# A layer of RWKV attention and a mixture of experts: expert tiles added to the output in DRAM, instead of written aside and gathered

## The chip, the cores and the metric

The kernel runs on one core of one Trainium2 chip. The metric is the device time of one execution in microseconds, the median of several runs. The profile is one execution with the hardware profiler; its times are microseconds from the first instruction, unless marked ns. The engines are TensorE (PE, with its weight loads PEld), VectorE (DVE), ScalarE (ACT), GpSimd (POOL) and SyncE (SP). Each of them works through its own queue of instructions in order. SyncE, ScalarE and GpSimd also issue DMA transfers.

## The reference

For 2048 tokens of 512 float32 numbers, the output is the input, plus an attention branch, plus a branch of routed experts. Both branches read the same normalised input.

```python
x = L0_attn_x                      # (1, 2048, 512)
xn = layernorm(x)
out = x + attention(xn) + experts(xn)

# attention: a recurrence over all tokens for each of 512 channels
# (tokens are 8 sequences of 256 only in the weights' setup; here one sequence of 2048)
r, v, k = split(xn @ W_rvk.T)
# step over t, with w = -exp(time_decay), u = time_first:
#   no = max(o, u + k);  A = exp(o - no);  Bc = exp(u + k - no)
#   y = (A * p + Bc * v) / (A * q + Bc)
#   no2 = max(w + o, k); p, q, o updated in the same manner with w
attention = (sigmoid(r) * y) @ W_out.T

# experts: 8 routed ones and 4 that return their input, the best 2 of 12 for each token
probs = softmax(xn @ classifier_w.T)
_, idx = top_k(probs + bias, 2)
rw = probs[idx] * 1.5
experts = sum over the 2 of: rw * (silu(xn @ gate.T) * (xn @ up.T)) @ down.T    # routed
                         or  rw * xn                                            # the other 4
```

## The kernel before

The kernel has five stages. It normalises x in four blocks of 512 tokens, stores the normalised rows (xs) in DRAM, and transposes each block. It computes the router and sorts tokens by expert: every expert gets whole tiles of 128 places, at most 40 tiles, of which the first 25 are always computed. It runs 16 units of the recurrence (wkv), one for each block and quarter of the channels. Between them it runs the expert tiles: each fetches its weights, gathers its 128 rows of xs by index, and stores 128 rows into ys in DRAM. After a branch for tiles 25 to 39, it combines: each tile of 128 tokens gathers two rows per token from ys, weighs and adds them to x and to the output projection. A scheduler decides the order in which each engine's instructions stand, so that the order of the text is a priority and not the order on the chip.

The pools, and the loads of x at the start:

```python
    xyp = pool("xy", 5)
    ewp = pool("ew", 3)
    rows = pool("rows", 4)
    rp = pool("route", 1)
    small = pool("small", 2)
    kvp = pool("kv", 2)
    wk = pool("wk", 2)
    ex_p = pool("exp", 2)
    # ...
    xs = dram.tile([T, C], F32, tag="xs", name="xs")
    ys = dram.tile([MAX_TILES * P, C], F32, tag="ys", name="ys")

    def load_x(i):
        t = rows.tile([P, C], F32, tag="ra", name=f"x{i}")
        nc.sync.dma_start(t, x[i * P : (i + 1) * P, :])
        xt[i] = t

    for i in range(NJ):
        load_x(i)
    # ... (classifier, bias, decay, first; constants on GpSimd)
```

The normalisation, the transposes and the router of one block, and the order of the loads:

```python
    def norm(b):
        js = slice(b * NJ, (b + 1) * NJ)
        for j in range(NJ):
            i = b * NJ + j
            st = small.tile([P, 6], F32, tag="st", name=f"st{i}")
            nc.vector.bn_stats(st, xt[i])
            nc.vector.bn_aggr(mv[:, i, :], st)
        var = mv[:, js, 1]
        ve = small.tile([P, NJ], F32, tag="ve", name=f"ve{b}")
        nc.vector.tensor_scalar_add(ve, var, EPS)
        # ... (variance, square root, reciprocal: rstd and shift)
        xn = []
        for j in range(NJ):
            i = b * NJ + j
            t = rows.tile([P, C], F32, tag="rb", name=f"xn{i}")
            nc.vector.tensor_scalar(t, xt[i], mv[:, i, 0:1], rstd[:, i : i + 1], ALU.subtract, ALU.mult)
            nc.scalar.dma_start(xs[i * P : (i + 1) * P, :], t)
            xn.append(t)
        xnT[b] = xyp.tile([P, CC, TB], F32, tag="xy", name=f"xnT{b}")
        for c in range(CC):
            pt = ps_tr.tile([P, TB], F32, tag="tr", name=f"pt{b}_{c}")
            for j in range(NJ):
                nc.tensor.transpose(pt[:, j * P : (j + 1) * P], xn[j][:, c * P : (c + 1) * P], ident)
            nc.scalar.copy(xnT[b][:, c, :], pt)
        for j in range(NJ):
            for c in range(CC):
                nc.tensor.matmul(
                    pl[:, b * NJ + j, :],
                    xnT[b][:, c, j * P : (j + 1) * P],
                    cls_sb[:, c, :],
                    start=(c == 0),
                    stop=(c == CC - 1),
                )

    norm(0)
    # ...
    for b in range(1, NTB):
        for j in range(NJ):
            load_x(b * NJ + j)
        if b == 1:
            load_w(2)
        norm(b)
    load_w(1)
    load_w(0)
    # ... (blank tiles of ys written from ACT's queue; the load of wout_sb)
```

The lists of tokens by place, after the choice of experts and the places (slot, low, high) are known; xa and xb carry what the input itself adds to the output:

```python
    NK = 2 * NT
    lowhot = xyp.tile([P, NK, P], BF16, tag="xy", name="lowhot")
    nc.vector.tensor_tensor(
        lowhot,
        lane.unsqueeze(1).to_broadcast([P, NK, P]),
        low.rearrange("p k j -> p (k j)").unsqueeze(2).to_broadcast([P, NK, P]),
        ALU.is_equal,
    )
    # ... (hh: is_equal of 40 tiles with high_b)
    tok = rp.tile([P, NK, 2, MAX_TILES], BF16, tag="tok", name="tok")
    nc.vector.tensor_tensor(
        tok[:, :, 0, :],
        hh,
        tok_j.rearrange("p k j -> p (k j)").unsqueeze(2).to_broadcast([P, NK, MAX_TILES]),
        ALU.mult,
    )
    nc.vector.tensor_scalar(tok[:, :, 1, :], hh, tok_p, None, ALU.mult)
    pi = ps_o.tile([P, 2, MAX_TILES], F32, tag="o", name="pi")
    for k in range(NK):
        nc.tensor.matmul(pi, lowhot[:, k, :], tok[:, k], start=(k == 0), stop=(k == NK - 1))
    pis = rp.tile([P, 2, MAX_TILES], F32, tag="pis", name="pis")
    nc.vector.tensor_copy(pis, pi)
    token_i = const.tile([P, MAX_TILES], I32, tag="token_i", name="token_i")
    nc.vector.scalar_tensor_tensor(token_i, pis[:, 0], float(P), pis[:, 1], ALU.mult, ALU.add)
    # ... (which expert a tile is of; wts, zero, xa, xb)
```

The expert tiles:

```python
    def fetch(i):
        # ... (e: the tile's expert)
        w = ewp.tile([P, CC, 2 * INTER], F32, tag="gw", name=f"gw{i}")
        nc.sync.dma_start(w, gu[bass.ds(e, 1)].rearrange("o p c n -> p (o c) n"))
        d = ewp.tile([P, IC, C], F32, tag="dw", name=f"dw{i}")
        nc.sync.dma_start(d, down[bass.ds(e, 1)].rearrange("o p c n -> p (o c) n"))
        xg = rows.tile([P, C], F32, tag="ra", name=f"xg{i}")
        nc.gpsimd.indirect_dma_start(
            out=xg,
            out_offset=None,
            in_=xs,
            in_offset=bass.IndirectOffsetOnAxis(ap=token_i[:, i : i + 1], axis=0),
        )
        st[i] = {"w": w, "d": d, "xg": xg}

    # turn: transposes xg; up: gate and up products, SiLU; turn_act: transposes act

    def finish(i):
        po = ps_o.tile([P, C], F32, tag="o", name=f"po{i}")
        for c in range(IC):
            nc.tensor.matmul(
                po, st[i]["actT"][:, c, :], st[i]["d"][:, c, :], start=(c == 0), stop=(c == IC - 1)
            )
        yo = rows.tile([P, C], F32, tag="rb", name=f"yo{i}")
        nc.scalar.copy(yo, po)
        nc.scalar.dma_start(ys[i * P : (i + 1) * P, :], yo)
        del st[i]

    def step(i, n):

        if i < n:
            up(i)
        if i > 0:
            turn_act(i - 1)
        if i + 1 < n:
            turn(i + 1)
        if i > 0:
            finish(i - 1)
        if i + 2 < n:
            fetch(i + 2)
```

The units of the recurrence, and how expert steps are put between them:

```python
    yT = {}

    def wkv(b, c):
        # ... (three projections on TensorE into ps_mm, copied or exponentiated by ACT into k, v, er;
        #      o, b and bv with their first columns copied on GpSimd; three scans, a reciprocal on VectorE;
        #      the result to yT[b][:, c, :])

    units = [(b, c) for b in range(NTB) for c in range(CC)]
    LEAD = 4
    for u in range(LEAD):
        wkv(*units[u])
    fetch(0)
    fetch(1)
    turn(0)
    done = 0
    for u in range(LEAD, len(units)):
        due = (u - LEAD + 1) * (TILES + 1) // (len(units) - LEAD)
        wkv(*units[u])
        while done < due:
            step(done, TILES)
            done += 1
    while done < TILES + 1:
        step(done, TILES)
        done += 1
```

The branch and the combine:

```python
    count = nc.values_load(
        which_i[0:1, MAX_TILES : MAX_TILES + 1],
        min_val=0,
        max_val=MAX_TILES,
        skip_runtime_bounds_check_because="a sum of E counts of at most 16, with 4096 places in all",
    )
    with tc.If(count > TILES):
        # ... (tiles 25 to 39)

    for i in range(NT):
        b, j = divmod(i, NJ)
        r = []
        for m, tag in ((0, "ra"), (1, "rb")):
            y = rows.tile([P, C], F32, tag=tag, name=f"y{m}_{i}")
            nc.gpsimd.indirect_dma_start(
                out=y,
                out_offset=None,
                in_=ys,
                in_offset=bass.IndirectOffsetOnAxis(ap=slot_i[:, m, i : i + 1], axis=0),
            )
            r.append(y)
        a = rows.tile([P, C], F32, tag="rc", name=f"acc{i}")
        nc.sync.dma_start(a, x[i * P : (i + 1) * P, :])
        nc.scalar.activation(a, a, AF.Identity, bias=xb[:, i : i + 1], scale=xa[:, i : i + 1])
        for m in range(2):
            nc.vector.scalar_tensor_tensor(a, r[m], wts[:, m, i : i + 1], a, ALU.mult, ALU.add)
        po = ps_o.tile([P, C], F32, tag="o", name=f"pw{i}")
        for c in range(CC):
            nc.tensor.matmul(
                po,
                yT[b][:, c, j * P : (j + 1) * P],
                wout_sb[:, c, :],
                start=(c == 0),
                stop=(c == CC - 1),
            )
        nc.vector.tensor_add(a, a, po)
        nc.sync.dma_start(out[i * P : (i + 1) * P, :], a)
```

## Time and profile before

| what | value |
|---|---|
| time, median of 3 runs | 461.27 us (459.91 to 467.19) |
| the profiled execution | 470.54 us, span 468.8 us |
| TensorE, VectorE, ScalarE, GpSimd busy | 414.4, 278.7, 125.2, 84.2 us |
| bytes moved by DMA | 86.08 MB, mean 184 GB/s |
| expert weights of one tile | 1024 KB landing in 6.9 us, 512 KB in 4.0 us (medians) |
| a 256 KB store to ys, a 256 KB load of x in the combine | 4.8 us, 2.7 us from issue to landing (medians) |

A float32 matmul stands in the profile as two passes, so 64 products of the output projection are 128 instructions. A row of the groups names the line, the engine and the operation, what is written and read with shapes, then the busy time, the mean of one instruction, and the idle time of its engine just before, with what ended it. Matmuls are pipelined, so the time from one start to the next says more than the length of one. The slices cut the span into 40 equal parts of 11.7 us; a digit is a busy share in tenths. A row of the waits names who waited for whom, the sum, how many times, and the longest.

### The profile page before, as it was taken

The numbers are of one execution on the slowest core, as the hardware profiler recorded it, in microseconds if no ns is written. First come the engines' busy times: TensorE is split into PE (matmuls) and PEld (weight loads), VectorE is DVE, ScalarE is ACT, GpSimd is POOL, SyncE is SP. The second block draws the span as 40 slices with busy tenths as digits, with TensorE's granted clock in tenths as the row PEclk, the third lists the DMA queues.
The fourth block names the chain that finished last, engine by engine and source line by source line (L and its number), as shares of the span: only waits on it lengthen the run. The fifth ranks groups of instructions, "written<-read, shape, count | busy, mean of one in ns | idle before, by whom it ended". The sixth has DMA issues, their size and how long they took to land. (4 is left out here: it accounts for less than half of the span.)

```text
span 468.8 us, 3952 instructions
## 1 busy us (share of the span) xinstructions
PE 414.4 (88%) x1204; PEld 201.8 (43%) x1204; DVE 278.7 (59%) x405; ACT 125.2 (27%) x227; POOL 84.2 (18%) x142
## 2 busy tenths in 40 slices
PE   0177999999898999999999999999999977849796
PEld 0053766444343444444444444444544433314332
DVE  4324523999999993756552837565574822534343
ACT  2042343222422433233223232332223320012120
POOL 3000000100542230111120101010100005754400
PEclk9998579899999999999999999999999998977899
DMA  7996520005650889274658383746544114886752
GB/s 236 412 362 223 181 90 1 0 0 228 242 159 0 260 293 325 88 291 127 231 181 291 111 314 91 269 144 214 177 161 159 65 48 119 276 269 222 215 160 109
DMA packets 27690, 86.08 MB, mean 184 GB/s; under 512 B 3792, under 2 KB 3792, under 8 KB 23952
## 3 DMA queue, kind: packets, MB, share of 16 engines
q1 hardware_dynamic: 15264, 56.14, 34.3%
q0 software_dynamic: 4560, 14.95, 10.8%
q10 hardware_dynamic: 7840, 14.68, 8.2%
q8 instruction: 12, 0.20, 0.2%
q14 instruction: 14, 0.11, 0.1%
HBM read 66.88 MB, written 18.87 MB: 183 GB/s over the span
## 5 line engine op out<-in xcount | busy, mean ns | idle before, releaser
L412 PE MATMUL pg<-gw,xgT 128*128 128x512 f32 x200 | 90.0, 593 | 0.0
L568 PE MATMUL pw<-wout_sb,yT 128*128 128x512 f32 x128 | 62.7, 650 | 16.1 <-DVE acc L575 12.0
L466 PE MATMUL pk<-xnT,wrvk 128*128 128x512 f32 x128 | 66.1, 632 | 0.0
L466 PE MATMUL pr<-xnT,wrvk 128*128 128x512 f32 x128 | 61.6, 619 | 0.0
L466 PE MATMUL pv<-xnT,wrvk 128*128 128x512 f32 x128 | 59.2, 597 | 0.9 <-ACT k L476 0.9
L412 PEld LDWEIGHTS pg<-gw,xgT 128*128 128x128 f32 x200 | 37.8, 190 | 47.7 <-issue 46.9
L509 DVE RECIPROCAL den<-den 128x512 f32<-128x512 f32 x16 | 53.6, 3349 | 0.3
L565 DVE SCALAR_TENSOR_TENSOR acc<-y,wts,acc 128x512 f32<-128x512 f32 x32 | 23.9, 751 | 41.9 <-ACT acc L563 19.7
L568 PEld LDWEIGHTS pw<-wout_sb,yT 128*128 128x128 f32 x128 | 26.1, 209 | 52.6 <-issue 35.6
L434 PE MATMUL po<-dw,actT 128*128 128x512 f32 x100 | 47.4, 596 | 1.4 <-ACT actT L428 1.2
L554 POOL DMA_INDIRECT y<-ys,slot_i x32 | 32.9, 1029 | 80.8 <-PEq L540 58.5
L393 POOL DMA_INDIRECT xg<-xs,token_i x25 | 28.2, 1127 | 86.3 <-PE px L404 71.0
L490 DVE TENSOR_TENSOR_SCAN obv<-wdec,state,k 128x512 f32<-128x512 f32 x16 | 20.3, 1277 | 37.5 <-ACT k L476 37.5
L466 PEld LDWEIGHTS pr<-xnT,wrvk 128*128 128x128 f32 x128 | 24.7, 198 | 28.6 <-issue 28.6
L466 PEld LDWEIGHTS pv<-xnT,wrvk 128*128 128x128 f32 x128 | 24.0, 192 | 29.2 <-issue 27.3
L174 PE MATMUL pt<-ident,xn 128*128 128x128 f32 x64 | 13.2, 354 | 25.2 <-ACT xnT L175 13.8
L418 DVE SCALAR_TENSOR_TENSOR th<-th,pg 128x256 f32<-128x256 f32 x25 | 9.8, 394 | 39.4 <-ACT th L417 39.4
L466 PEld LDWEIGHTS pk<-xnT,wrvk 128*128 128x128 f32 x128 | 24.1, 204 | 20.8 <-issue 20.8
L503 POOL COPY state<-obv 128x3 f32<-128x3 f32 x12 | 6.1, 511 | 139.9 <-DVE obv L500 137.4
L563 ACT ACTIVATE acc<-acc,xb,xa 128x512 f32<-128x512 f32 x16 | 12.8, 814 | 63.2 <-DMA acc<-in_x_dram 59.0
L499 DVE TENSOR_TENSOR_SCAN sums<-obv,state,a 128x512 f32<-128x512 f32 x16 | 20.5, 1279 | 15.5 <-ACT obv L495 14.9
L434 PEld LDWEIGHTS po<-dw,actT 128*128 128x128 f32 x100 | 18.7, 190 | 24.3 <-issue 17.0
(134 smaller groups left out, 401.1 us busy)
## 6 DMA issues: line engine op xcount, KB each, us to landing
gw<-in_gu_dram SPq DMA_DIRECT2D x25, 1024.0 KB, 6.9
dw<-in_down_dram SPq DMA_DIRECT2D x25, 512.0 KB, 4.0
ys<-yo ACTq DMA_DIRECT2D x25, 256.0 KB, 4.8
x<-in_x_dram SPq DMA_DIRECT2D x16, 256.0 KB
xs<-xn ACTq DMA_DIRECT2D x16, 256.0 KB, 7.4
acc<-in_x_dram SPq DMA_DIRECT2D x16, 256.0 KB, 2.7
out_dram<-acc SPq DMA_DIRECT2D x16, 256.0 KB
ys<-blank ACTq DMA_DIRECT2D x1, 3840.0 KB
```

The lines of the kernel that those rows point to most:

```text
L174: nc.tensor.transpose(pt[:, j * P : (j + 1) * P], xn[j][:, c * P : (c + 1) * P], ident)
L393: nc.gpsimd.indirect_dma_start(out=xg, out_offset=None, in_=xs, in_offset=bass.IndirectOffsetOnAxis(ap=token_i[:, i : i + 1], axis=0),)
L412: nc.tensor.matmul(pg, st[i]["xgT"][:, c, :], st[i]["w"][:, c, :], start=(c == 0), stop=(c == CC - 1))
L434: nc.tensor.matmul(po, st[i]["actT"][:, c, :], st[i]["d"][:, c, :], start=(c == 0), stop=(c == IC - 1))
L466: nc.tensor.matmul(ps, wrvk_sb[m][:, k, c * P : (c + 1) * P], xnT[b][:, k, :], start=(k == 0), stop=(k == CC - 1),)
L490: nc.vector.tensor_tensor_scan(o2, w.to_broadcast([P, TB]), k, s[:, 0:1], ALU.add, ALU.max)
L499: nc.vector.tensor_tensor_scan(sq, bs, a2, s[:, 3:4], ALU.add, ALU.mult)
L509: nc.vector.reciprocal(den, den)
L554: nc.gpsimd.indirect_dma_start(out=y, out_offset=None, in_=ys, in_offset=bass.IndirectOffsetOnAxis(ap=slot_i[:, m, i : i + 1], axis=0),)
L563: nc.scalar.activation(a, a, AF.Identity, bias=xb[:, i : i + 1], scale=xa[:, i : i + 1])
L565: nc.vector.scalar_tensor_tensor(a, r[m], wts[:, m, i : i + 1], a, ALU.mult, ALU.add)
L568: nc.tensor.matmul(po, yT[b][:, c, j * P : (j + 1) * P], wout_sb[:, c, :], start=(c == 0), stop=(c == CC - 1),)
```

## The change

Each expert tile's rows are multiplied by their weight of routing in the evacuation of PSUM, and an indirect DMA adds them to the rows of the output in DRAM. Tokens occur once in a tile; empty places point to 128 spare rows past the end. For this the place lists carry the weights too, as a sum of three bfloat16 parts. What the combine did is split: x times its factor is written to the output before the experts ("base"), and the output projection is added by an accumulating DMA once its block of the recurrence is done. Nothing is left after the branch, so the branch comes last. The purpose is to free the end of the kernel of its gathers and to let the output projection stand between the other matmuls.

Two further parts: x is loaded whole, into buffers that are used by others later, instead of four tiles at a time, with the stores of xs issued by SyncE; and the router multiplies with the 32-wide padded classifier as the stationary side, its four slices of the contraction in four column groups of TensorE, which a second small product adds up. k, v and er have three buffers instead of two.

The diff, cut to its core:

```diff
     keep = pool("keep", 1)
     xyp = pool("xy", 5)
     ewp = pool("ew", 3)
+    gathered = pool("gathered", 3)
     rows = pool("rows", 4)
+    basep = pool("base", 2)
     rp = pool("route", 1)
     small = pool("small", 2)
-    kvp = pool("kv", 2)
+    kvp = pool("kv", 3)
     wk = pool("wk", 2)
     ex_p = pool("exp", 2)
     dram = pool("dram", 1, space=bass.MemoryType.DRAM)
# ... (cut)
+    def load_x(b):
+
+        if b < 3:
+            t = ewp.tile([P, NJ, C], F32, tag="gw", name=f"x{b}")
+        else:
+            t = xyp.tile([P, NJ, C], F32, tag="xy", name=f"x{b}")
+        for j in range(NJ):
+            i = b * NJ + j
+            nc.sync.dma_start(t[:, j, :], x[i * P : (i + 1) * P, :])
+            xt[i] = t[:, j, :]
+
# ... (cut)
+    load_x(0)
+    cls_sb = const.tile([P, CC, QW], F32, tag="cls", name="cls_sb")
     nc.sync.dma_start(cls_sb, cls)
+    load_x(1)
+    load_w(2)
+    load_x(2)
     nc.sync.dma_start(bias_sb, ebias.partition_broadcast(P))
+    load_w(1)
+    load_x(3)
+    load_w(0)
+    wout_sb = keep.tile([P, CC, C], F32, tag="wout", name="wout_sb")
+    nc.sync.dma_start(wout_sb, w_out)
# ... (cut)
-            nc.scalar.dma_start(xs[i * P : (i + 1) * P, :], t)
+            nc.sync.dma_start(xs[i * P : (i + 1) * P, :], t)
# ... (cut)
+        lg = ps_tr.tile([P, TB], F32, tag="tr", name=f"lg{b}")
+        for c in range(CC):
+            nc.tensor.matmul(
+                lg[c * QW : (c + 1) * QW, :],
+                cls_sb[:, c, :],
+                xnT[b][:, c, :],
+                start=True,
+                stop=True,
+                tile_position=(0, c * QW),
+            )
+        lgs = small.tile([P, TB], F32, tag="lgs", name=f"lgs{b}")
+        nc.scalar.copy(lgs, lg)
         for j in range(NJ):
-            for c in range(CC):
-                nc.tensor.matmul(
-                    pl[:, b * NJ + j, :],
-                    xnT[b][:, c, j * P : (j + 1) * P],
-                    cls_sb[:, c, :],
-                    start=(c == 0),
-                    stop=(c == CC - 1),
-                )
+            nc.tensor.matmul(
+                pl[:, b * NJ + j, :], lgs[:, j * P : (j + 1) * P], quarters, start=True, stop=True
+            )
# ... (cut)
+    for n in range(3):
+        part = rp.tile([P, 2, NT], BF16, tag=f"part{n}", name=f"part{n}")
+        nc.vector.tensor_copy(part, wts)
+        parts.append(part)
+        if n < 2:
+            nc.vector.tensor_sub(wts, wts, part)
# ... (cut)
+        tok = ewp.tile([P, NT, NV, MAX_TILES], BF16, tag="gw", name=f"tok{m}")
+        for v, a in ((0, tok_j[:, m]), (2, parts[0][:, m]), (3, parts[1][:, m]), (4, parts[2][:, m])):
+            eng = nc.vector if v in (0, 2) else nc.gpsimd
+            eng.tensor_tensor(
+                tok[:, :, v, :], hh, a.unsqueeze(2).to_broadcast([P, NT, MAX_TILES]), ALU.mult
+            )
+        nc.vector.tensor_scalar(tok[:, :, 1, :], hh, tok_p, None, ALU.mult)
# ... (cut)
+    nc.vector.tensor_scalar(token_i, token, -float(P), 0.0, ALU.add, ALU.max)
+    empty = rp.tile([P, MAX_TILES], F32, tag="empty", name="empty")
+    nc.vector.tensor_scalar(empty, token, float(P), spare, ALU.is_lt, ALU.mult)
+    to_i = const.tile([P, MAX_TILES], I32, tag="to_i", name="to_i")
+    nc.vector.scalar_tensor_tensor(to_i, token, -float(P), empty, ALU.add, ALU.add)
+    wplace = const.tile([P, MAX_TILES], F32, tag="wplace", name="wplace")
+    nc.vector.tensor_add(wplace, pis[:, 3], pis[:, 4])
+    nc.vector.tensor_add(wplace, wplace, pis[:, 2])
# ... (cut)
     nc.vector.tensor_mul(xb, xa, shift)
     nc.vector.tensor_mul(xa, xa, rstd)
     nc.vector.tensor_scalar_add(xa, xa, 1.0)
+
+
+    blank = basep.tile([P, C], F32, tag="base", name="blank")
+    nc.gpsimd.memset(blank, 0.0)
+    nc.sync.dma_start(out[T:, :], blank)
+    for i in range(NT):
+        a = basep.tile([P, C], F32, tag="base", name=f"base{i}")
+        nc.sync.dma_start(a, x[i * P : (i + 1) * P, :])
+        nc.scalar.activation(a, a, AF.Identity, bias=xb[:, i : i + 1], scale=xa[:, i : i + 1])
+        nc.sync.dma_start(out[i * P : (i + 1) * P, :], a)
 
 
     st = {}
# ... (cut)
-        nc.scalar.copy(yo, po)
-        nc.scalar.dma_start(ys[i * P : (i + 1) * P, :], yo)
+        nc.scalar.activation(yo, po, AF.Identity, scale=wplace[:, i : i + 1])
+        nc.gpsimd.indirect_dma_start(
+            out=out,
+            out_offset=bass.IndirectOffsetOnAxis(ap=to_i[:, i : i + 1], axis=0),
+            in_=yo,
+            in_offset=None,
+            compute_op=ALU.add,
+        )
# ... (cut)
+    def attention(b):
+        for j in range(NJ):
+            i = b * NJ + j
+            # ... (as before: four products into po)
+            a = rows.tile([P, C], F32, tag="rb", name=f"att{i}")
+            nc.scalar.copy(a, po)
+            nc.gpsimd.dma_start(out[i * P : (i + 1) * P, :], a, accum_op=ALU.add)
# ... (cut)
-        due = (u - LEAD + 1) * (TILES + 1) // (len(units) - LEAD)
-        wkv(*units[u])
+        due = (u - LEAD + 1) * (TILES + 1 - LAST) // (len(units) - LEAD)
+        b, c = units[u]
+        wkv(b, c)
+        if c == 0:
+            attention(b - 1)
         while done < due:
             step(done, TILES)
             done += 1
     while done < TILES + 1:
         step(done, TILES)
         done += 1
+
+    attention(NTB - 1)
# ... (cut)
# (the loop of the combine after the branch goes)
-    args.append(nc.dram_tensor("out_0_dram", (T, C), F32, kind="ExternalOutput").ap())
+    args.append(nc.dram_tensor("out_0_dram", (T + P, C), F32, kind="ExternalOutput").ap())
-    return r.results[0]["out_0_dram"].reshape(1, T, C)
+    return r.results[0]["out_0_dram"][:T].reshape(1, T, C)
```

The loads, the base stores and the weights of the experts all leave from SyncE's queue; gathers, scatters and the accumulating DMAs of the attention leave from GpSimd's.

## The prediction

> **What bounds the kernel now.** I read the page's busy row and slices first, then the table of stretches, the groups, the waits and the end of the timeline. The first fence is from the page: TensorE's busy tenths, its granted clock, DMA's share.
>
> ```profile
> PE 414.4 (88%) x1204; PEld 201.8 (43%) x1204; DVE 278.7 (59%) x405; ACT 125.2 (27%) x227; POOL 84.2 (18%) x142
> ...
> PE   0177999999898999999999999999999977849796
> ...
> PEclk9998579899999999999999999999999998977899
> DMA  7996520005650889274658383746544114886752
> ```
>
> TensorE is the bound in the middle and not at the two ends. The stretches say the same in microseconds (columns: busy PE, PE weight load, DVE, ACT, POOL, then clock, DMA share, GB/s):
>
> ```profile
> 10.00:20.00 10.00, 1.97 (x8) 1.19 (x8) 4.63 (x14) 0.82 (x2) 0.00 (x0) 1.00 1.01 390
> 20.00:30.00 10.00, 3.58 (x15) 3.07 (x16) 2.55 (x11) 4.17 (x7) 0.00 (x0) 1.00 1.03 416
> ...
> 250.00:300.00 50.00, 50.00 (x139) 23.68 (x138) 28.48 (x34) 15.43 (x31) 7.48 (x11) 1.00 0.63 215
> ...
> 390.00:469.00 79.00, 62.41 (x128) 25.79 (x127) 33.37 (x48) 9.79 (x12) 32.92 (x32) 0.89 0.63 200
> ```
>
> So the ledger must be one of TensorE time. In the steady loop eight passes of a 128x512 matmul start 3.43 us after the eight before (139.82 to 143.25), 0.429 us each; the 593 ns of the group rows overlap. At that pace: 384 projection passes 164.9, 200 expert up passes 85.8, 100 expert down 42.9, 128 output-projection passes 54.9, 150 expert transposes 16.3 (four in 0.43, two in 0.22), 64 transposes of xn 7.0, 128 router passes at 0.114 (28 in 3.19) 14.6, index matmuls 2.5. Sum 389 us. The span of 468.8 minus 414.4 busy gives 54 us idle; the other 25 us of busy time are low clock and pipeline ends.
>
> Where the 54 idle us lie: 28 before 50 us, 4 between 130 and 386, 22 after that, a few between. The waits name them:
>
> ```profile
> PE pt L174 <- ACT xnT L175: 13.8, 2, 13.3
> PE pw L568 <- DVE acc L575: 12.0, 4, 6.2
> PE pt L174 <- DVE xn L167: 11.4, 2, 11.1
> PE pw L568 <- PEq L540: 4.1, 1, 4.1
> ```
>
> The 13.3 us wait is not ACT at work. The timeline shows ACT's queue issuing stores:
>
> ```profile
> 15.59 10.15 ACTq L168 DMA_DIRECT2D xs<-xn  x4
> ```
>
> Four issues that take 0.33 us each elsewhere took 10 us while the DMA engines stood at a share of 1.01; the PSUM copies stood behind them. The end is the combine: 16 tiles from 389.7 to 464.4, 4.7 us each where 8 passes need 3.43. Its pace is set on SyncE, where an x load waits for the store that frees its buffer and the next store stands behind that load:
>
> ```profile
> SPq L562 <- DMA out_dram<-acc: 33.8, 10, 5.5
> ```
>
> **What the Trainium skill says.** "DMA: Bandwidth & Descriptors", section "SWDGE vs HWDGE vs iDMA": accumulation during a DMA is only to be had from GpSimd. The trace before has no accumulating DMA; its gathers cost GpSimd 0.97 to 1.03 us each. The same page, "Rules for kernel authors": an accumulate reads its destination and writes later, with nothing held in between, so the next one on the same bytes must wait for its semaphore. No run here shows it yet, but a scatter's rows are known only at run time, so all scatters must form one chain. "Collectives: The Full Stack", section "The bandwidth ceiling: the fold count and why AG ≠ RS ≠ AR": an add in a DMA costs a second source read, not adder cycles. Not in this trace either. "TensorE: Matmul & The Clock Gate", section "Part 3: Packing small matmuls — row/col tiling": three column tiles at N=512 ran 2.38 times as fast. The old router has none.
>
> **The change part by part.**
>
> Output projection moved. Its 54.9 us of passes now run between the wkv units, where the old loop left TensorE idle for only 4 us; they are not hidden, they shift the loop's end by 55 us. What goes is the stretch 386 to 469, 83 us, so 28 us net, of which 4 are the branch gap ahead of the combine and 8 low clock.
>
> New tail. After the last pw: an ACT copy 0.6, GpSimd's issue about 1.1, landing. A plain 256 KB store takes 4.8 us from issue to landing (ys), a gather 3.8 to 6 (chain). With a second read I estimate 5 to 6. That makes about 8 us, against 4.4 from the last pw to the old end; the branch, 4.1 us, runs on the other engines beside that landing. Cost 4, net so far 24 us.
>
> Front. x goes to buffers of its own and the xs stores to SyncE, so the 13.3 us wait goes; the first 11.1 us (load, statistics, square root) stay. Loads of x after block 0 used to wait for freed row buffers (norm of block 3 ended near 67 us). Now four blocks of norm need DVE about 6.4 us each, some 26 in all, so norms end near 35 to 40. I count 13 us saved here and no more: DVE takes over, with routing (about 23 us of its own instructions between 81 and 121, lowhot's 4.42 the longest) and wkv (12.3 us a unit against TensorE's 10.3). The third k/v/er buffer lets TensorE run three units ahead. DVE by 80 us can do norm 26, routing 27, two units; TensorE then has five units to do, about 52 us, which about fills it. Indices ready near 80 instead of 121.
>
> Router. 14.6 us become 32 passes of 512 columns in four groups: 13.7/2.4 = 5.7 by the page's three-tile speedup, plus 32 small passes at 0.114, 3.6. Saved 5.
>
> Routing extra. Two more products on DVE (640 elements, about 0.75 each by half of tok's 1.49), four on GpSimd in parallel, wider pi (200 columns instead of 80), casts of 0.17: 4 to 5 us longer on the index path, with TensorE busy on wkv meanwhile. Zero on the end, or up to 3.
>
> Base. 16 loads, 16 ACT instructions of 0.81, 16 stores, two buffers, all after routing. By the combine's pattern a tile costs a store's landing, about 4.5: 72 us, say from 80 to 152. It is beside TensorE work, but no scatter may start before it ends; four output buffers then fill and GpSimd stands at the first scatter. I book 8 us of TensorE stalls.
>
> Scatter chain. 25 scatters, each issue 1 plus landing 5 to 6, about 6.5 us: 163. Four groups of four attention accumulates, disjoint rows: 4x1.1 plus 6, about 10 each: 40. Together 203 us in the 240 between 152 and TensorE's end. It fits with 15% to spare. Gathers and the small state copies stand behind these waits on GpSimd; the old loop had them free (POOL busy 7.5 of 50). Three gathered buffers cover one scatter's wait. I book 4 us more.
>
> DVE loses the combine's 32 products and 16 adds, 23.9 + about 11 us; off the path. DRAM traffic: ys blank 3.8 MB, ys stores 6.5 and gathers 8.4 go; 10.8 MB of accumulates come, read and written.
>
> Sum on the profile's scale: 389 - 5 = 384 of passes, idle at the start 16, in the loop 4 + 12, tail 8, low clock about 10 of the former 25: 434. By differences: 469 - 24 - 13 - 5 + 12 = 439. The profiled execution took 470.54 where the timed median is 461.27, a factor 0.98: 425 to 430. I predict 428.
>
> **Rivals.**
>
> One: the accumulate chain becomes the bound. If a scatter takes 9 us or more, 25x9 + 4x13 = 277 from 152 is 429, plus tail: 437 to 445; at 11 us, 152 + 275 + 60 = 487, slower than before. For it: the DMA engines are already at 0.63 in the loop and share with 1 MB weight loads. Against it: gathers occupied an engine only 0.9 us each (10.8% of 468.8 over 57 transfers), so a doubled one leaves room.
>
> Two: base and the waits on GpSimd hold TensorE. Expert weights leave on the same SyncE queue as base; ACT stands in order at each base load. Were the loop to start only when base is done, TensorE idles some 30 us and the kernel ends near 450. Against it: seven wkv units are free of all that.
>
> Three: the front gains little since DVE was 100% busy from 80 to 120 anyway; the gain of 13 shrinks to 5 and the time is 436.
>
> Four, better: stalls I booked don't occur and the clock stays full, 410.
>
> **Range and chances.** 428, with 408 to 456 for eight in ten: below lies rival four, above a slow chain or a late loop. Faster by over 2% means under 452.0: only rival one in its worse form or two in full exceed that, 0.82. Within 2%: 0.09. Slower, a chain at 11 us: 0.09.
>
> **What would show it.** Right: TensorE's second and third slices filled, xg's first gather near 80, PE tenths at 9 through to the last two slices, pw between the wkv units, the last chain an accumulate of att after pw, about 8 us. Wrong: GpSimd waiting on DMA out for more than half the loop with TensorE waiting for xg or yo (chain too slow); ACT waiting on base loads while projections stand; scatters still going long after the last matmul; or SyncE's queue holding gw behind base stores. If accumulates land in over 9 us, the prediction fails on that term.

## Result and the profile after

The changed kernel takes 441.18 us (median of 4 runs, 440.21 to 442.26) against 460.59 us before (4 runs, 458.21 to 467.19): a ratio of 0.9596, 95% interval 0.9545 to 0.9646. A second set of five runs gave 441.09 us and 0.9572 (0.9502 to 0.9642). The prediction was 428 us, between 408 and 456.

The execution of the kernel before that the prediction read took 470.5 us; a second one, with a span of 460.5 us ("before, again" below), stands in for it from here on.

From the page of the changed kernel: TensorE's busy time, its tenths in 40 slices, the granted clock and DMA's share.

```profile
PE 394.0 (90%) x1140; PEld 185.3 (42%) x1140; DVE 254.0 (58%) x372; ACT 130.0 (30%) x241; POOL 110.6 (25%) x160
...
PE   0599999768997999999999999999999999999970
...
PEclk9999999997999999999999999999999999999995
DMA  8946302177794859694676666666568483935371
```

The second slice is filled, the slices of the old combine are gone, and the last slice and part of the one before it are empty. TensorE is idle for 438.3 - 394.0 = 44 us. The waits name most of it (in all, times, longest):

```profile
PE pt L202 <- DVE xn L195: 12.3, 2, 11.7
PE po L481 <- ACT actT L475: 4.7, 4, 3.0
PE pt L202 <- ACT xnT L203: 4.5, 1, 4.5
PE px L451 <- DMA xg<-xs,token_i: 4.3, 1, 4.3
PE pi L372 <- DVE tok L369: 3.6, 2, 2.3
```

The first and third are the start, 17 us. The fourth and fifth are the index path between 83 and 100 us. Most of the second lies near 140 us: ACT's copy of actT stands in ACT's queue behind an instruction of the base tiles that waits for its load:

```profile
138.22 1.63 ACT L421 ACTIVATE base<-base,xb,xa 128x512 f32<-128x512 f32 x2 [2.58 <-DMA base<-in_x_dram]
...
140.44 1.98 PE L481 MATMUL po<-dw,actT 128*128 128x512 f32 x4 [2.98 <-ACT actT L475]
```

The steady loop, and for comparison the stretch where indices and base are busy (columns: busy PE, PE weight load, DVE, ACT, POOL, clock, DMA share, GB/s):

```profile
80.00:100.00 20.00, 12.11 (x54) 6.29 (x53) 20.00 (x33) 4.44 (x7) 11.20 (x9) 0.94 0.47 159
...
160.00:380.00 220.00, 220.00 (x595) 103.12 (x594) 115.79 (x132) 63.87 (x123) 65.79 (x65) 1.00 0.66 181
```

From 160 to 380 us TensorE never stops, although GpSimd stands 44.8 of these 220 us waiting for its own accumulates. From the groups and from GpSimd's waits:

```profile
L486 POOL DMA_INDIRECT out_dram<-yo,to_i x25 | 41.0, 1638 | 100.2 <-DMA out_dram<-yo,to_i 50.9
```
```profile
POOL out_dram L486 <- DMA out_dram<-yo,to_i: 50.9, 10, 6.4
```

An accumulating scatter costs GpSimd 1.6 us to issue and lands 6.7 us after its issue began (medians; the attention's accumulates 0.86 and 4.1). The 25 of them are issued from 162.7 to 414.6 us, and no wait of TensorE is put down to that chain.

The end of the changed kernel, in order of time, and then the closing instructions of GpSimd's queue (form: count, ns min/median/max, start):

```profile
423.41 1.02 PE L572 MATMUL pw<-wout_sb,yT 128*128 128x512 f32 x2
424.51 0.59 ACT L580 COPY att<-pw 128x512 f32<-128x512 f32 x1 [2.85 <-PE pw L572]
425.39 0.85 POOL L581 DMA_DIRECT2D out_dram<-att  x1 [2.58 <-ACT att L580]
```
```profile
L615 POOLq INC_SWDGE_SEM  x1: 1499/1499/1499, 430.2 to 430.2; - x1
```
```profile
L660 POOLq DRAIN  x3: 46/113/5460, 431.7 to 437.7; - x3
```

From the last pass to the end are 13.9 us: copy and issue 1.8, the landing to 430.2, then 1.5 us of a semaphore instruction and 5.46 us of a drain on GpSimd, then the last barrier. Before, GpSimd's drain began at 436.8 us and lay beside the combine; only 4.4 us followed the last pass.

### The profile page after: what moved, and what is told of

Same layout as the page of the kernel before. It is cut to its first block, busy times and chain, and to the rows that moved or that the text cites. A ratio compares the mean times of both kernels' runs of the same rounds, so it can differ in the third digit from the quotient of the medians.

```text
span 438.3 us, 3781 instructions
## 1 busy us (share of the span) xinstructions
PE 394.0 (90%) x1140; PEld 185.3 (42%) x1140; DVE 254.0 (58%) x372; ACT 130.0 (30%) x241; POOL 110.6 (25%) x160
## 3 DMA queue, kind: packets, MB, share of 16 engines
q0 software_dynamic: 7904, 17.31, 22.4%
## 4 chain that ended last, share of the span: by engine, by line
PE 68%; DVE 12%; DMA 10%; issue 3%; ACT 3%; POOL 1%; SPq 0%; POOLq 0%; ACTq 0%; DVEq 0%
PE pg L459 18%; PE po L481 10%; PE pr L519 9%; PE pv L519 9%; PE pk L519 8%; PE pw L572 7%; DMA base<-in_x_dram 4%; DMA out_dram<-base 3%; PE px L451 2%; DMA xg<-xs,token_i 1%; DVE xn L195 1%; DMA out_dram<-yo,to_i 1%; PE pt L202 1%; DVE lowhot L347 1%; PE lg L207 1%
## 5 line engine op out<-in xcount | busy, mean ns | idle before, releaser
L486 POOL DMA_INDIRECT out_dram<-yo,to_i x25 | 41.0, 1638 | 100.2 <-DMA out_dram<-yo,to_i 50.9
L519 PE MATMUL pk<-xnT,wrvk 128*128 128x512 f32 x128 | 61.9, 594 | 0.0
L519 PE MATMUL pr<-xnT,wrvk 128*128 128x512 f32 x128 | 60.0, 608 | 0.0
L519 PE MATMUL pv<-xnT,wrvk 128*128 128x512 f32 x128 | 58.1, 592 | 0.0
L572 PE MATMUL pw<-wout_sb,yT 128*128 128x512 f32 x128 | 56.0, 594 | 0.0
L572 PEld LDWEIGHTS pw<-wout_sb,yT 128*128 128x128 f32 x128 | 24.5, 192 | 31.4 <-issue 30.7
L485 ACT ACTIVATE yo<-po,wplace 128x512 f32<-128x512 f32 x25 | 17.2, 687 | 46.9 <-PE po L481 46.9
L519 PEld LDWEIGHTS pk<-xnT,wrvk 128*128 128x128 f32 x128 | 22.2, 191 | 18.9 <-issue 18.9
L464 ACT ACTIVATE th<-pg 128x256 f32<-128x256 f32 x25 | 9.6, 382 | 67.3 <-PE pg L459 67.3
L202 PE MATMUL pt<-ident,xn 128*128 128x128 f32 x64 | 11.7, 318 | 17.1 <-DVE xn L195 12.3
```

Of the source, the lines that this page charges most:

```text
L485: nc.scalar.activation(yo, po, AF.Identity, scale=wplace[:, i : i + 1])
L486: nc.gpsimd.indirect_dma_start(out=out, out_offset=bass.IndirectOffsetOnAxis(ap=to_i[:, i : i + 1], axis=0), in_=yo, in_offset=None, compu ...
L519: nc.tensor.matmul(ps, wrvk_sb[m][:, k, c * P : (c + 1) * P], xnT[b][:, k, :], start=(k == 0), stop=(k == CC - 1),)
L572: nc.tensor.matmul(po, yT[b][:, c, j * P : (j + 1) * P], wout_sb[:, c, :], start=(c == 0), stop=(c == CC - 1),)
```

## Experiments

Times are medians; each ratio is to runs of the kernel before on the same chip in the same session, with medians of 462.14, 461.20, 461.76 and 463.54 us in the four sessions; the ratios leave out the slowest of these runs, so they are not the quotients of the medians. Two or three microseconds between two of these kernels are not separated by the intervals.

**The kernel before, again.** No edit. 

> The kernel before, profiled once more, to have a ledger of an execution at the usual time. Theory (my sum was right, but taking the 0.98 off the changed kernel was wrong): span about 457 to 460, the 9 us less than in the first profile lie in TensorE's busy time at a higher granted clock or in idle time at the start and end, and the steady loop from 130 to 386 us is unchanged within 1 us. Rival (the gain is smaller because the loop of the kernel before is better than the profile showed): the 9 us lie in the loop.

462.32 us in one run, span 460.5 us. The indices are ready, and the first gather issued, at 113.6 us, the first pass of the combine at 382.1 us after a branch wait of 4.3; so from the loop's end, 377.8, to the end are 82.7 us. That confirms the 83 us of the prediction. In the execution that it read, the first gather was issued at 121.3 us; these 8 us are nearly the whole difference of the two spans, and from there on the two run alike.

**The branch taken out.**

```diff
-    with tc.If(count > TILES):
-        for i in range(TILES, MAX_TILES):
-            fetch(i); turn(i); up(i); turn_act(i); finish(i)
```

It leaves out the surplus tiles, of which this input has none. 

> The changed kernel with the branch and its tiles 25 to 39 left out; nothing else. Theory (the 14 us between the last matmul and the end are mostly GpSimd's own closing work, which the branch lengthens: the wait at the join, the counting of its DMA semaphores and the last drain): 4 to 6 us less, 435 to 437, with the last accumulate landing as before. Rival (the tail is the landing of the last accumulate): less than 1.5 us changes.

439.05 us, 0.9528 (0.9466 to 0.9589). The tail fell from 13.9 to 8.7 us, but the last pass ended at 427.4, 3 us later: the wait for actT was 5.5 instead of 4.7 us, and the granted clock between 80 and 120 us was 0.83 and 0.91 (by 20 us; 0.94 and 0.89 in the changed kernel). The total moves by 2 us. The branch stands on the tail for about 5 us; what it is worth in the total is not separated from such scatter.

**Plain writes.** `compute_op=ALU.add` and `accum_op=ALU.add` are dropped, so tiles overwrite one another and nothing is summed. 

> The changed kernel with scatters and the attention's stores as plain writes of the same bytes, the adding left out; waits and order as they are. Theory (the chain of accumulates is hidden): the landing of a scatter falls from 6.7 to about 5 us and the time stays within 2 us of the changed kernel. Rival (the chain and the waits on GpSimd hold the loop): 8 us less or more.

434.12 us, 0.9402 (0.9344 to 0.946). The scatter's issue falls from 1.58 to 0.98 us (medians), the direct write's from 0.86 to 0.55; the direct writes land in 2.4 us instead of 4.1. The time GpSimd stands at its writes to the output, waiting for a scatter to land, falls from 54.7 to 34.1 us and TensorE's last pass moves by only 1.4 us. The medians differ by 7 us. TensorE ran through the loop in both, so most of it does not come through the chain. The profile of "the changed kernel, again" below, an execution of 443.28 us, shows 6.9 us of difference in its span to this one: its last pass ends at 426.8 (here 423.0) and its tail is 14.7 us (here 11.6). The tail's part is the last write, which has landed 6.5 us after the last pass there and 3.4 here. The other part is mostly the wait for actT, 4.4 us there and 1.8 here. ACT waits for loads of base tiles for 11.9 us there and 9.3 here; that the attention's adding beside them makes these loads late is an inference.

**All the output projection after the loop.**

```diff
-        if c == 0:
-            attention(b - 1)
...
-    attention(NTB - 1)
+    for b in range(NTB):
+        attention(b)
```

> The changed kernel with all four blocks of the output projection after the last expert step, still accumulated into the output. Theory (TensorE's passes are the bound and it does not matter where the 128 passes stand): 0 to 4 us more, 441 to 445. Rival (the gain comes from filling the loop with the projection's passes): 10 us more or worse, with idle TensorE between the units.

439.27 us, 0.951 (0.9449 to 0.957). Where the 128 passes stand makes no difference that these runs resolve: they are 55 us of a bound engine in either place. What the change gained there it gained by replacing the old combine, not by mixing.

**The changed kernel, again.** No edit. 

> The changed kernel once more, so that the others of this call can be held against it on one chip: 438 to 443, a ratio of 0.955 to 0.965 to the kernel before.

441.09 us, 0.9572, as above.

**The last four tiles added on VectorE.**

```diff
+            if b < NTB - 1:
                 nc.gpsimd.dma_start(out[i * P : (i + 1) * P, :], a, accum_op=ALU.add)
+                continue
+            # load the four tiles of out, tensor_add on VectorE, store from SyncE
```

> The changed kernel with the last block of the output projection (4 tiles) added on VectorE to the output's rows, loaded back after the last scatter, and stored by SyncE; the other 12 tiles accumulate as before. Theory (GpSimd's closing work, about 7 us from its last landing to the last barrier, stands at the end, because GpSimd issues the last DMA): GpSimd's closing begins at the last scatter's landing and ends before the stores, the span ends 4 to 6 us after the last matmul, 8 us less, about 432 to 434. Rival (the tail is the DMA's landing and the drains are fixed, whoever issues): within 2 us of the changed kernel.

438.90 us, 0.953 (0.9445 to 0.9616). GpSimd's drain now starts at 425.2 us, beside TensorE's last passes, and the tail is 9.1 us; the last pass ended at 427.9. The net is 2 us, not the 8 expected.

**The old router in the changed kernel.** The four-column-group passes, the copy and the 32 small passes are replaced by the 128 passes of 12 columns of before. 

> The changed kernel with the router of the kernel before (128 passes with xn as the stationary side). Theory (7 us of TensorE's passes saved at a place where TensorE is the bound): 4 to 8 us more, 445 to 449. Rival (the router's passes lie where VectorE's chain to the indices is the limit): within 2 us.

453.45 us, 0.9857 (0.9746 to 0.9969): 12 us lost, where the passes themselves are only 5. At 0.114 us each the 128 passes are 14.6 us. In the changed kernel the column-group passes of the four blocks are these:

```profile
20.11 2.64 PE L207 MATMUL lg<-xnT,cls_sb 128*32 128x512 f32 x8
...
39.58 1.07 PE L207 MATMUL lg<-xnT,cls_sb 128*32 128x512 f32 x8
...
45.57 1.79 PE L207 MATMUL lg<-xnT,cls_sb 128*32 128x512 f32 x8
...
52.61 1.26 PE L207 MATMUL lg<-xnT,cls_sb 128*32 128x512 f32 x8
```

To the start of what follows they are 2.57, 1.00, 1.72 and 1.19 us, and with four times 0.81 for the small passes 9.7. Only in the second block did all four groups start together at full pace. The timeline shows where the rest is. TensorE in the kernel with the old router:

```profile
18.53 1.97 PE L202 MATMUL pt<-ident,xn 128*128 128x128 f32 x8 [4.53 <-ACT xnT L203]
...
23.30 5.56 PE L207 MATMUL pl<-cls_sb,xnT 128*128 128x12 f32 x26
28.71 5.47 PE L512 MATMUL pk<-xnT,wrvk 128*128 128x512 f32 x6
...
45.16 1.04 PE L202 MATMUL pt<-ident,xn 128*128 128x128 f32 x8
...
47.34 3.19 PE L207 MATMUL pl<-cls_sb,xnT 128*128 128x12 f32 x28
50.38 4.38 PE L512 MATMUL pv<-xnT,wrvk 128*128 128x512 f32 x6
```

Six projection passes took 5.47 us; the next group starts at 33.97, so 0.88 us each, where the loop needs 0.43; and the 26 router passes 0.21 each, where the 28 from 47.34 us took 3.19, 0.114 each. Nothing is waited for. The half pace is older than the narrow passes: the eight transposes ahead of them took 1.97 us, and eight later ones 1.04. It lasts until 34.4 us, in the changed kernel only until 22.6; half of these 12 us is lost. It comes back once: the six passes after the 28 from 47.34 us take 0.70 us each, 1.6 us lost. After the narrow passes of the third and fourth block the pace stays full. With the 5 us of passes these losses are 12.5.

**The narrow router passes made wide.**

```diff
-QW = 32
+QW = 128            # the weights padded with zeros from 12 to 128 columns
...
-    (column groups, copy, small products)
+    (128 passes xnT x padded weights, then a copy of 12 of 128 columns)
```

> The changed kernel with the router of the kernel before, but its moving side padded from 12 to 128 columns, so that each of the 128 passes streams as much as a transpose; the sums go through a PSUM bank of their own and one small ACT copy. The pace of a pass was set by its weight load and should stay near 0.115 us. Theory (narrow passes let TensorE's clock down, and the projections after them run at half pace): projections after the router's passes at 0.43 us instead of 0.85, about 5 us less than with the narrow router, 447 to 450. Rival (the low pace after the router has another cause): same as the narrow router, 452 to 455, with passes of 0.85 us after it.

447.46 us, 0.9692 (0.9636 to 0.9748): half of the loss is back, with as many router passes that each do ten times the work. The logits of all blocks then lie in SBUF, not in PSUM. The same place in TensorE's timeline:

```profile
21.69 3.77 PE L204 MATMUL pb<-cls_sb,xnT 128*128 128x128 f32 x29
25.29 3.60 PE L510 MATMUL pk<-xnT,wrvk 128*128 128x512 f32 x8
```

Full pace comes within the router's own passes. What is left of the loss, 6 us, is about what the passes need: 15.1 us in place of 9.7. The Trainium skill, "TensorE: Matmul & The Clock Gate", section "Part 1: The HAM clock gate (the "warmup" mystery)", says that TensorE's clock is halved until a window of activity has been busy, and names two paces in the ratio of two. The pace agrees (0.88 against 0.43), and so does the trace's record of the clock. The first entry of that record is the rise to full clock, at 34.4 us with the narrow router, 22.4 with the wide one, 22.6 in the changed kernel and 42.8 in the kernel before, again; a clock of 1.00 printed for a time ahead of it is the lack of an entry and no reading. Where the half pace comes back after the second block's narrow passes, the record has it:

```profile
51.50:55.00 3.50, 3.50 (x7) 1.36 (x7) 2.60 (x4) 0.00 (x0) 0.00 (x0) 0.51 0.66 250
```

Shown is that with passes of 12 columns the half pace of the start lasted 12 us longer and came back after the passes of one of three later blocks, and that with passes of 128 columns neither happened. That narrow passes count as too little activity is an inference from the two runs.

**The front alone in the kernel before.** x loaded whole, key/value buffers 2 to 3, xs stored from SyncE instead of ACT's queue, the weights loaded between the blocks of x.

```diff
-    kvp = pool("kv", 2)
+    kvp = pool("kv", 3)
...
-            nc.scalar.dma_start(xs[i * P : (i + 1) * P, :], t)
+            nc.sync.dma_start(xs[i * P : (i + 1) * P, :], t)
...
+    for j in range(NJ):      # load_x(b): whole blocks, issued ahead of the norms
```

> The kernel before with the changed loading alone: x whole in buffers of its own, the stores of xs on SyncE, k, v and er in three buffers (and one shared scratch buffer for the index constants, to make room). Router, combine and branch as before. Theory (the front is worth what I booked, 13 us, less what VectorE takes back): 8 to 13 us less than the kernel before, 448 to 453. Rival (VectorE's index chain is the limit and takes it all): within 3 us of the kernel before.

461.02 us in 20 runs, 1.0042 (1.0008 to 1.0077). The front, for which the prediction booked 13 us, is worth nothing by itself.

**The front and the column router in the kernel before.** 

> The kernel before with the changed loading, three k, v and er buffers and the router in four column groups; combine and branch as before (the list of products for the indices lies in a weight buffer, to make room). What the changed kernel has beyond this is the scatters, base, the moved output projection and the branch at the end. Theory (the router with the front carries most of the gain and the scatters little): 447 to 451, so that the scatter part is worth 6 to 10 us. Rival (my prediction's split, router 5, front 13, scatters 24 less 12): 441 to 445 here, or 456 and more if the front stays worth nothing.

460.90 us in 20 runs, 1.0004 (0.9975 to 1.0033). Still nothing, although 5 us of the router's passes are gone. One wait had appeared:

```profile
PE pl L213 <- ACT lgs L211: 11.3, 1, 11.3
```

ACT stood there for the statistics of the last block, and these for the last loads of x. SyncE's queue in this kernel, the loads of the last block (start, time to issue four):

```profile
13.05 16.45 SPq L92 DMA_DIRECT2D x<-in_x_dram  x4
```

Issues that take 0.45 us each elsewhere took until 29.5 us. In the same time the kernel before, and this one, write 3840 KB of zero tiles to ys, in one transfer, here issued at 7.4 us (KB, us to landing):

```profile
ys<-blank ACTq DMA_DIRECT2D x1, 3840.0 KB, 20.8
```

The changed kernel has no ys, and so no such transfer: a part of the change that the prediction names only as traffic that goes.

**The zero tiles moved into the loop.** As the last, with the transfer cut into 15 stores.

```diff
-    nc.scalar.dma_start(
-        ys[TILES * P :, :].rearrange("(t p) c -> p t c", p=P),
-        blank.unsqueeze(1).to_broadcast([P, MAX_TILES - TILES, C]),
-    )
...      # in step(i, n):
+        t = TILES + i - 4
+        if i >= 4 and t < MAX_TILES:
+            nc.sync.dma_start(ys[t * P : (t + 1) * P, :], blank)
```

> The kernel before with the front (x whole, three key/value buffers, xs stores on SyncE) and the column-group router, as in front_router, but with the 3.84 MB of blank tiles of ys no longer stored in one transfer in the first 30 us: tile by tile, one 256 KB store at each of the 15 loop steps 4 to 18, from SyncE. Theory A (the DMA engines were the bound of the front: in front_router they run at 0.89 for the first 40 us, and the last loads of x, issued from 13 us, were held until 29.5): the transfer is 3.84 MB at about 400 GB/s = 9.6 us, and the start shortens by 8 to 11 us: the last block's loads are through near 20 instead of 29.5, the PE wait of 11.3 us for lgs falls to under 3, px comes near 100 instead of 109, the loop ends near 372 instead of 381 and the total is 450 to 454, against 460.9 in front_router. Rival B (the gain is given back in the loop and the combine: the loop's end did not move when px came 3 to 8 us earlier): px earlier, but the last loop pass still at 380 to 382 and the total 459 to 462. Rival C (ACT's queue, held by issuing the one large store, and not the DMA engines, was what stalled): the same gain as A, but the loads of x would then still run to 29 us and only ACT's copies come earlier.

445.66 us (6 runs, 444.66 to 446.83), 0.9681 (0.9624 to 0.9738), 15 us less than with the transfer at the start. The loads of the last block are issued in 4 us:

```profile
10.00 4.19 SPq L92 DMA_DIRECT2D x<-in_x_dram  x4
```

The wait for lgs is gone, the first px moves from 109.3 to 94.0 us, the first pass of the combine from 381.0 to 365.7. Part of this is pace: here TensorE is at full clock from 22.4 us, there, after the wait for lgs, only from 41.6. The first 40 us of four kernels, in this order: before again, front and router, zero tiles moved, and the changed kernel (columns as above):

```profile
0.00:40.00 40.00, 14.76 (x61) 12.43 (x62) 13.37 (x40) 8.17 (x12) 4.42 (x47) 1.00 0.92 330
```
```profile
0.00:40.00 40.00, 11.76 (x38) 6.39 (x39) 17.98 (x66) 6.57 (x13) 5.36 (x50) 0.85 0.89 322
```
```profile
0.00:40.00 40.00, 22.31 (x83) 11.13 (x87) 28.11 (x80) 11.94 (x22) 7.26 (x52) 1.00 0.76 283
```
```profile
0.00:40.00 40.00, 23.05 (x83) 11.15 (x87) 28.52 (x81) 11.94 (x22) 7.77 (x55) 1.00 0.76 284
```

The last two are the same start. DMA at 0.9 held TensorE and VectorE; with 3840 KB less, both do half as much again or more. The rival that ACT's queue was what the one large store held falls, since loads from SyncE's queue were what came earlier. The rival that the loop gives the gain back falls too. This kernel also frees a buffer that the zero tile had held; no wait of TensorE in the kernel without the move is put down to that buffer. The move alone, with the old loads and router, was not tried.

This kernel does one thing more: it comes near the changed kernel without its scatters, base tiles and added index products. It waits in the combine as the kernel before does:

```profile
PE pw L583 <- DVE acc L590: 10.8, 6, 3.7
...
PE pw L583 <- PEq L555: 2.7, 1, 2.7
PE pa L436 <- DVE act L430: 2.6, 1, 2.6
PE po L444 <- ACT actT L438: 1.3, 2, 0.7
```

**A version better than both.** The changed kernel with the four index products that were GpSimd's on VectorE, four base buffers instead of two, and the last four tiles as in the experiment above.

```diff
-    basep = pool("base", 2)
+    basep = pool("base", 4)
...
-            eng = nc.vector if v in (0, 2) else nc.gpsimd
+            eng = nc.vector
```

> A version to beat both: the changed kernel with all products of the token lists on VectorE, four base buffers instead of two, and the last block of the output projection added on VectorE and stored by SyncE. Theory (GpSimd's products slow VectorE's on the path to the indices; base loads hold ACT near 140 us; GpSimd's closing stands at the end): first gather 2 to 4 us earlier, the wait of po for actT under 1.5 us, tail 9 us instead of 14: 432 to 436. Rival (each gap moves elsewhere): 438 to 441.

428.98 us (6 runs, 428.17 to 432.57), 0.9294 (0.925 to 0.9339), 12 us below the changed kernel. The waits for tok are gone, the wait for actT is 1.3 us, the first px comes at 97.1, the last pass ends near 419, the tail is 11.3. What each of the three parts gives is not separated, but for the last, which alone gave 2 us. From 80 to 100 us, against 12.11 us of TensorE in the changed kernel:

```profile
80.00:100.00 20.00, 17.11 (x69) 8.99 (x68) 20.00 (x38) 7.83 (x13) 5.86 (x6) 1.00 0.52 180
```

That VectorE's instructions are longer beside GpSimd's products shows in the changed kernel's timelines. GpSimd's four products, and VectorE's instructions before, beside and after them:

```profile
80.18 6.88 POOL L366 TENSOR_TENSOR tok<-hh,part 128x640 bf16<-128x640 bf16 x4 [12.17 <-DVE part L338]
```
```profile
79.08 0.19 DVE L341 TENSOR_TENSOR wts<-wts,part 128x32 f32<-128x32 f32 x1
...
80.74 1.28 DVE L341 TENSOR_TENSOR wts<-wts,part 128x32 f32<-128x32 f32 x1
...
84.58 1.37 DVE L369 TENSOR_SCALAR tok<-hh,tok_p 128x640 bf16<-128x640 bf16 x1
...
88.41 0.37 DVE L369 TENSOR_SCALAR tok<-hh,tok_p 128x640 bf16<-128x640 bf16 x1
```

The same instruction on the same size takes 1.0 to 1.1 us longer while GpSimd works. The skill's "GPSIMD Engine Reference", section "8. Key points", says that the two engines share their interfaces to SBUF and that VectorE's instructions with two inputs, or in a two-port mode, contend; the trace agrees, though two products of 0.81 us in between kept their length.

## Why the prediction was right, and where it was not

The direction and the range held. The number, 428, was 13 us too low, and some of its terms were right for the wrong reason.

**The ledger.** "TensorE is the bound in the middle and not at the two ends" held, and the sum by passes and idle times, 434, came within 4 us of the measured span of 438.3. Its terms against the trace: passes 384, now about 384 (384 projection passes at 0.429 us are 164.7, not 164.9); start 16, now 17; loop 16, now 13; tail 8, now 14; low clock 10, now about 10 (394.0 busy less 384). **The step that failed is the last one**, "a factor 0.98: 425 to 430". It took 8 us off terms that the shorter execution of the kernel before has too: a pass takes 0.429 us there, the two waits at the start 14.1 and 11.2, the stretch after the loop 82.7. The other term that missed is the tail, 6 us too small. That the sum by differences, 439, met the span was luck: it began 8 us too high, at 469 where the second execution has 460.5, and took off 30 where 22 came.

**Output projection and combine, -24.** The old stretch of 83 us was right (82.7), but the arithmetic was not: the stretch to the end at 469 already holds the old tail of 4.4 us, so the whole new tail of 8 is to be charged, not the difference of 4. That makes -20. With the tail as it is, -14 or so. Working it against the kernel with the zero tiles moved, which has the same start: its loop ends at 365.7 - 2.7 = 363.0, its end is 443.3, 80.3 us. The changed kernel puts 54.9 us of passes after that point, 417.9, ends its passes at 424.4, 6.5 us of stalls, and has 13.9 of tail: 80.3 - 54.9 - 6.5 - 13.9 = 5.0 us gained, the difference of the two spans, where the prediction had 24 - 12 = 12. By the medians the accumulating scatters are worth 4 to 5 us; the intervals of the two ratios, 0.9596 and 0.9681, overlap, so the size is not sharp.

**New tail, 8.** Measured 13.9. The copy, the issue and the landing came to 5.8 us, less than the 8 booked. What the prediction had not listed is GpSimd's closing work: 1.5 and 5.46 us that before lay hidden behind the combine, and that an accumulate as the last transfer pushes out to the end.

**Front, -13.** Neither the size nor the cause was right. The 13.3 us wait of ACT's store issues does go, and is worth nothing alone (1.0042) nor with the router (1.0004): with the DMA engines still full, the wait moves to the next one in line. The 10 us issue that the prediction read as ACT's queue at fault was the DMA engines' load; the prediction even wrote the share of 1.01 beside it. It counted the blank tiles as traffic and gave them no time, and they are 3840 KB in a start where DMA is the bound. With them out of the start, the front and router together are worth 15 us of 18 predicted. But of these 15 the router is worth 12, going by what its return cost the changed kernel, so some 3 are left for the front and the zero tiles together, an estimate from two different kernels; the front in such a start without the new router was not tried. Rival three, "the front gains little", came nearest, with 5 us and 436; the reason that it gave, a full VectorE, was not tested apart.

**Router, -5.** The passes were foreseen right: 9.3 us in place of 14.6, and 9.7 measured. Measured in the total with the start free are 12, and the other 7 are half pace, which nothing in the prediction foresaw; its table reads a clock of 1.00 from 10 to 30 us, where that execution's record has no entry before 30.9 and its transposes ran at half pace. In a start bound by DMA the router is worth nothing.

**Routing extra, 0 to 3.** It was on the path: TensorE waits 3.6 us for tok and 4.3 for the first gather. The indices were ready at 94, not 80; against 113.6 before that is 19 us earlier, not 41.

**Base, 8 of stalls; scatter chain, 4.** The base stores ended at 158 us for a predicted 152 and the first scatter went out at 162.7. Of the 12 us booked here, 3.4 came: the wait for actT, against the kernel without base tiles (4.7 against 1.3). With the 3.6 for tok that is 7.0, about the 6.5 us of stalls above. The chain cost TensorE nothing in the loop: 220 of 220 us. Landing was 6.7 us for "about 6.5". Rival one falls by this; rival two in full falls, and in its small form is those 3.4 us; rival four, 410, did not come, and the version with most stalls removed still takes 429.

**What stays open.** What makes the loads of base tiles late where the attention's writes add. What of the 15 us at the start the zero tiles and the front are worth without the new router. And which of its three parts makes the better version better.

## What to carry to other kernels

When the issue of a store is slow, look at the DMA share beside it before blaming the queue: if the engines are full, moving the issue moves the wait, and only bytes taken out of that stretch help, however useless the transfer looks. Charge a new last transfer with everything that its engine does to close, not only with its landing, and end on an engine whose closing work can be done earlier. And a time summed from passes needs no factor for the scale of the profile they were read in.

## What the runs showed of the hardware

- TensorE starts at half pace (0.88 us instead of 0.43 for 512 columns). With router passes of 12 columns this lasted until 34.4 us and came back once after them, from 51.5 to 55.0 us; with passes padded to 128 columns it ended at 22.4 us and did not come back after them.
- An accumulating 256 KB write costs GpSimd 0.3 us more to issue as a plain transfer (0.86 against 0.55) and 0.6 us more as a scatter (1.58 against 0.98), and the direct one lands 1.7 us later (4.1 against 2.4).
- GpSimd's end of work after its last transfer has landed takes 7 us (1.5 and 5.46; 1.4 and 5.13 where its last transfer was a scatter).
- Beside elementwise work on GpSimd some of VectorE's instructions took 1.0 to 1.1 us longer each, others no longer.
- Eight passes of 512 columns in four column groups took 1.00 us in the block where the groups started together, 3.4 times as fast as eight one after the other (3.43); in the two later blocks they took 1.72 and 1.19.
